# Turning h with VectorE and DRAM in place of TensorE transposes, with the pieces in another order

## The chip, the cores and the metric

The kernel runs on one core of one Trainium2 chip. The metric is the device time of one execution in microseconds. The 32 inputs of the batch are called graphs. "Per graph" is the period of the steady state, read from the starts of equal instructions in neighbouring graphs.

## The reference

Two layers, each with a residual and a layer normalisation, over 32 graphs of 512 nodes with 512 features, all in fp32:

```python
# layer 0: graph convolution, W = [Wi | Wj]
out = deg[None, :, None] * (x @ Wi.T + b) + einsum('ij,bjo->bio', a, x @ Wj.T)
h = layernorm(x + out)
# layer 1: attention over the edges, 8 heads of 64
q, k, v = (split_heads(h @ W.T + bias) for W, bias in ...)
scores = where(adj == 0, -inf, q @ k^T / 8)
out = softmax(scores) @ v
y = layernorm(h + merge_heads(out) @ Wo.T + bo)
```

The step at issue lies between the layers. q, k and v contract over the features of h, so they need h with the features on the partitions; layer 0 leaves it with the nodes there. h has to be turned.

## The kernel before

Every 512x512x512 product is done in seven quarter products (`piece` 1 to 7) instead of eight. Some pieces take a quarter of their operand as it is (1, 2, 3), the others a sum of quarters that GpSimd has made (`combos`: t1 for piece 5, t2 for 6, t3 for 7, t4 for 4). Below, l0-3 is piece 3 of layer 0, pj is the projection by Wo, and v1, q5 and so on are pieces of v and q. Piece by piece, two PSUM banks ("mma" and "mmb") take turns. The copy or sum that takes a finished piece out of its bank is its eviction.

The kernel is a software pipeline in which all engines work in program order. While the attention of graph n-1 runs in eight steps, the pieces of other graphs fill the steps: layer 0, then v, q and k of graph n, pj of graph n-2, and the start of layer 0 of graph n+1. A step is cut from one list by weights; an entry made with `z` weighs nothing, as it is work for the other engines:

```python
def by_steps(todo):
    total, done, at, res = sum(f[0] for f in todo), 0.0, 0, []
    for step in range(STEPS):                       # 8
        res.append([])
        while at < len(todo) and (done < total * (step + 1) / STEPS - 1e-6 or step == STEPS - 1):
            res[-1].append(todo[at]); done += todo[at][0]; at += 1
    return res
# main loop, cut
for step in range(STEPS):
    scores(b, hp, 2 * half); scores(b, hp, 2 * half + 1)   # TensorE; ScalarE exp; VectorE mask product -> e
    ... values(b, ph, phalf) ...; sums(b, ph)              # TensorE, with the e of the step before
    for f in PERIODS[n][step]:
        run(f)                                             # a piece, or a z entry
        ...                                                # after a piece: reciprocals, scale, check, sum of e
```

Two things follow for every step. The two mask products of its `scores` come first in VectorE's order, ahead of everything that the step's list gives to VectorE. And what they make is read by TensorE only in the next step. "e" is the exponentials of the scores times the edge mask; its sum is the denominator of the softmax, and the "check of sums" is a VectorE instruction on these denominators.

h was turned in the kernel before by TensorE, four 128x128 transposes for each of four row groups, through a PSUM tile that is also one of the two score tiles:

```python
def l0_norm(b, ic):
    y = XT[b][:, ic, :]
    if ic == 0:
        HT[b] = big()
    pt = turn_tile()
    for dc in range(DC):
        nc.tensor.transpose(pt[:, dc * P:(dc + 1) * P], y[:, dc * P:(dc + 1) * P], ident)
    nc.scalar.copy(HT[b][:, :, ic * P:(ic + 1) * P], pt.rearrange("p (c i) -> p c i", c=DC))
```

x was already turned by VectorE in 32x32 blocks, with a load from DRAM (`load_xa`) that puts each block where its transpose belongs.

## Time and profile before

| | before |
|---|---|
| median time | 3837.6 us |
| span of the profiled run | 3835.8 us |
| TensorE busy | 99% |
| one graph, by starts | 117.64 us |
| transposes of h on TensorE per graph, by starts | 1.82 us |

How to read the lines in this document. PE is TensorE, DVE VectorE, ACT ScalarE, POOL GpSimd; L339 is line 339 of that run's kernel. In the groups by shape, the columns are line, engine, operation, output and inputs, shapes and count, then busy time and mean length in ns, then the idle time just before and what ended it. In the timeline they are start, length, engine, line, operation and count, with the idle time before it and its releaser in brackets. Matmuls overlap, so the price of one on TensorE is the distance of starts and not its length. From the groups of the kernel before, the ScalarE copy after the transposes and the turn of x on VectorE:

```profile
L339 ACT COPY big<-sc 128x512 f32<-128x512 f32 x128 | 72.0, 592 | 150.9 <-PE sc L338 150.9
L324 DVE STREAM_TRANSPOSE big<-xa 128x512 f32<-128x512 f32 x124 | 85.6, 691 | 0.0
```

512 columns on VectorE cost 0.69 us beside TensorE, while the way through TensorE also costs ScalarE 0.59 us per row group.

### The profile page before, as it was taken

How to read it: one execution, taken by the hardware profiler on the slowest of the kernel's cores; microseconds unless marked ns; L12 is line 12 of the kernel's file. 1: busy time of each engine (PE TensorE's matmuls, PEld its weight loads, DVE VectorE, ACT ScalarE, POOL GpSimd, SP SyncE). 2: the span in 40 equal slices, each digit the busy share in tenths (PEclk: the TensorE clock that was granted, in tenths of full speed). 3: DMA queues.
4: the chain of work that ended last, by engine and by line, in shares of the span. 5: the costliest groups of instructions: out<-in, count | busy, mean ns of one | idle time of the engine just before them, and what ended most of it. 6: DMA issues, size and time to landing. Idle time of an engine off the chain costs nothing.

```text
span 3835.8 us, 46277 instructions
## 1 busy us (share of the span) xinstructions
PE 3794.4 (99%) x16906; PEld 2595.5 (68%) x16906; DVE 2587.3 (67%) x3520; ACT 1064.0 (28%) x1476; POOL 1990.0 (52%) x1985
## 2 busy tenths in 40 slices
PE   8999999999999999999999999999999999999997
PEld 5666767676767676667666666667666767676663
DVE  4667666676766666666767676676667676666765
ACT  2222232222332223322223222232222232222222
POOL 4455544555545555445555455554555554555523
PEclk9999999999999999999999999999999999999998
DMA  7434444444444344434444443444434444444330
GB/s 250 131 99 130 124 124 123 118 113 124 126 124 127 99 129 124 127 120 110 121 128 119 127 126 105 124 127 122 129 99 129 126 121 124 123 111 121 116 110 32
DMA packets 537798, 466.33 MB, mean 122 GB/s; under 512 B 279008, under 2 KB 375776, under 8 KB 537568
## 3 DMA queue, kind: packets, MB, share of 16 engines
q1 hardware_dynamic: 537312, 462.78, 41.7%
q8 instruction: 138, 2.26, 0.2%
q14 instruction: 92, 0.75, 0.1%
q0 software_dynamic: 256, 0.53, 0.0%
HBM read 421.80 MB, written 41.42 MB: 121 GB/s over the span
## 4 chain that ended last, share of the span: by engine, by line
PE 92%; DVE 5%; ACT 1%; DMA 1%; issue 1%; POOL 0%; SPq 0%; POOLq 0%; DVEq 0%; ACTq 0%
PE mmb L393 29%; PE mma L393 29%; PE sc L445 12%; PE ov L466 11%; PE mmb L310 3%; PE mma L310 3%; PE ov L473 3%; DVE e L450 2%; PE sc L338 1%; DVE st L274 1%; DVE es L458 1%; ACT sc L449 1%; DVE rl L488 1%; DVE xh L411 0%; DVE mv L275 0%
## 5 line engine op out<-in xcount | busy, mean ns | idle before, releaser
L449 ACT ACTIVATE sc<-sc 128x1024 f32<-128x1024 f32 x512 | 492.9, 1007 | 1357.2 <-PE sc L445 1353.0
L450 DVE TENSOR_TENSOR e<-sc,edge 128x1024 f32<-128x1024 f32 x512 | 602.5, 1218 | 374.6 <-ACT sc L449 374.6
L393 PE MATMUL mmb<-ring,big 128*128 128x256 f32 x3144 | 728.6, 380 | 0.2 <-ACT big L339 0.2
L393 PE MATMUL mma<-ring,big 128*128 128x256 f32 x3112 | 721.4, 380 | 4.9 <-ACT p L400 3.0
L393 PEld LDWEIGHTS mmb<-ring,big 128*128 128x128 f32 x3144 | 593.8, 190 | 105.5 <-issue 25.9
L393 PEld LDWEIGHTS mma<-ring,big 128*128 128x128 f32 x3112 | 587.6, 190 | 110.2 <-issue 25.2
L362 POOL TENSOR_TENSOR big<-big 128x512 f32<-128x512 f32 x376 | 524.8, 1424 | 205.7 <-ACT big L316 165.0
L445 PE MATMUL sc<-q,k 64*128 64x512 f32 x2048 | 509.7, 616 | 0.0
L466 PE MATMUL ov<-e,v 128*64 128x512 f32 x2048 | 496.1, 605 | 5.8 <-DVE oT L498 5.8
L488 DVE RECIPROCAL rl<-ov 128x128 f32<-128x128 f32 x512 | 459.3, 928 | 15.3 <-PE ov L473 6.0
L393 PE MATMUL mma<-big,ring 128*128 128x256 f32 x1808 | 434.4, 383 | 1.4 <-DVE k L436 0.2
L393 PE MATMUL mmb<-big,ring 128*128 128x256 f32 x1776 | 427.1, 383 | 2.1 <-DVE k L427 0.8
L276 POOL TENSOR_SCALAR mv<-mv 128x1 f32<-128x1 f32 x256 | 49.5, 193 | 724.2 <-DVE mv L275 714.0
L325 POOL TENSOR_TENSOR big<-big,deg_r 128x512 f32<-128x512 f32 x124 | 157.4, 1269 | 512.4 <-DVE big L324 512.4
L393 PEld LDWEIGHTS mma<-big,ring 128*128 128x128 f32 x1808 | 337.2, 190 | 83.2 <-issue 24.3
L393 PEld LDWEIGHTS mmb<-big,ring 128*128 128x128 f32 x1776 | 330.9, 190 | 84.5 <-issue 26.0
L466 PEld LDWEIGHTS ov<-e,v 128*64 128x64 f32 x2048 | 124.6, 136 | 345.9 <-issue 270.8
L456 POOL TENSOR_TENSOR es<-e 128x1024 f32<-128x1024 f32 x128 | 301.7, 2357 | 76.9 <-PE ov L473 63.8
L458 DVE TENSOR_TENSOR es<-es,e 128x1024 f32<-128x1024 f32 x248 | 319.5, 1288 | 0.0
L445 PEld LDWEIGHTS sc<-q,k 64*128 64x128 f32 x2048 | 176.7, 186 | 207.9 <-issue 207.9
L193 POOL TENSOR_TENSOR xlo<-xh,xhi 128x512 fp32r<-128x512 f32 x128 | 163.4, 1287 | 213.3 <-ACT xhi L192 213.3
L408 POOL TENSOR_TENSOR xh<-xh,p 128x512 f32<-128x512 f32 x186 | 231.8, 1273 | 45.8 <-ACT sc L449 39.0
(147 smaller groups left out, 3702.0 us busy)
## 6 DMA issues: line engine op xcount, KB each, us to landing
ring<-wq SPq DMA_DIRECT2D x160, 256.0 KB, 2.7
ring<-wv SPq DMA_DIRECT2D x160, 256.0 KB, 2.6
ring<-wk SPq DMA_DIRECT2D x160, 256.0 KB, 2.8
ring<-wi SPq DMA_DIRECT2D x155, 256.0 KB, 2.8
ring<-wj SPq DMA_DIRECT2D x155, 256.0 KB, 2.6
ring<-wo SPq DMA_DIRECT2D x155, 256.0 KB, 2.6
xh<-in_x_dram SPq DMA_DIRECT2D x32, 1024.0 KB, 5.4
xa<-in_x_dram SPq DMA_DIRECT2D x124, 256.0 KB, 3.8
```

Source lines behind the costliest of these rows:

```text
L193: nc.gpsimd.tensor_sub(lo, xs, hi.bitcast(FT))
L310: nc.tensor.matmul(pm, parts[w][:, jc, :], adjR[:, jc, :], start=(w == 0 and jc == 0), stop=(w == 1 and jc == NC - 1))
L362: nc.gpsimd.tensor_tensor(dst, p, q, op=OP.subtract)
L393: nc.tensor.matmul(pm[:, c * Q:(c + 1) * Q], lhs, rhs, start=first, stop=(kc == 1 and n == len(terms) - 1), skip_group_check=True)
L408: nc.gpsimd.tensor_tensor(d, d, p1, op=OP.add)
L445: nc.tensor.matmul(ps[:, s, :], KT[b, hp // 2][r, hp % 2, kc * P:(kc + 1) * P], QT[b, hp // 2][r, hp % 2, :], start=True, stop=True)
L449: nc.scalar.activation(ps, ps, AF.Exp, scale=QSCALE)
L450: nc.vector.tensor_tensor(e, ps, edge[:, kc:kc + 1, :].to_broadcast([P, 2, N]), op=OP.mult)
L456: nc.gpsimd.tensor_add(ES[hp], E[0], E[1])
L458: nc.vector.tensor_add(ES[hp], ES[hp], E[half])
L466: nc.tensor.matmul(PV[hp][s * HD:(s + 1) * HD, :], V[b][:, kc, c0:c0 + HD], E[kc][:, s, :], start=(kc == 0), stop=(kc == NC - 1))
L488: nc.vector.reciprocal(rl[:, c], pl[:, c])
```

## The change

The intent is to take the transposes off TensorE, the bound engine. From graph 2 on, each normalised half of h (256 rows) is stored to DRAM by the ScalarE queue, loaded back by four transfers that put every 32x32 block in its place, and turned by VectorE with one instruction of 1024 columns. That way is long, so the pieces are put in an order in which work stands between the end of layer 0 and the first piece that needs h. The turns and loads of x move to later steps.

```diff
+    def h_store(b, half):
+        if half == 0:
+            HR[b] = dram.tile([N, D], FT, name="hd", bufs=2)
+        nc.scalar.dma_start(rows(HR[b])[:, 2 * half:2 * half + 2, :], XT[b][:, 2 * half:2 * half + 2, :])
+
+    def h_load(b, half):
+        if half == 0:
+            HA[b] = work([P, DC, N], "xa", 1).rearrange("p (n c) (d i) -> p n (c d) i", n=2, d=2)
+        src = HR[b].rearrange("(t p) (c q f) -> q p c t f", p=32, q=4, f=32)
+        for q in range(4):
+            nc.sync.dma_start(HA[b][32 * q:32 * q + 32, half].rearrange("p c (t f) -> p c t f", f=32),
+                              src[q][:, :, 8 * half:8 * half + 8, :])
+
+    def h_turn(b, half):
+        if half == 0:
+            HT[b] = big()
+        nc.vector.transpose(HT[b][:, :, Q * half:Q * half + Q], HA[b][:, half])
...                                     (piece: the bias of q and k at another visit, because of the new order)
+    LATE = (5, 3, 6, 7, 4)
...                                     (start of layer 0: k in the order LATE, the turns of x here)
 phase_b, graphs 2 to 31:
+        return [l0[2], *project(m, 1), l0[6], *project(m, 2), l0[7], z(add_bo, n - 1, 0), *project(m, 6), l0[4], z(stats, n, 0),
+                *project(m, 7), z(apply, n, 0), z(h_store, n, 0), l0[5], z(add_bo, n - 1, 1), *project(m, 4), z(h_load, n, 0),
+                l0[3], z(stats, n, 1), z(stats, m, 0), *project(m, 5)]
 phase_c, graphs 2 to 31:
+            res = [z(h_turn, n, 0), z(apply, n, 1), z(h_store, n, 1), v[1], *project(m, 3), z(stats, m, 1), v[2], q[1],
+                   z(h_load, n, 1), k[1], z(apply, m, 0), z(apply, m, 1), q[2], z(store, m), k[2], z(h_turn, n, 1),
+                   z(combos, TH, n, h, (1, 2)), z(combos, TH, n, h, (3, 4))]
...                                     (then q and v in the order LATE, with the loads of the next x)
```

More of the change, by code (lines that the diff above doesn't have):

```diff
@@ L96, in turn_tile @@
         return sc_tile()[:, 0, :]
+    HA, HR = {}, {}
     XT, XA, XD, AX_T, HT, MV = {}, {}, {}, {}, {}, {}
@@ L411, in piece @@
                 nc.vector.tensor_tensor(d, d, pm, op=OP.add)
-        elif kind == "v":
-            if i == 1:
-                V[b] = work([P, NC, D], "v", 2)
-            d = quarter(V[b], n, f)
-            if i == 2:
-                nc.scalar.copy(d, pm)
-            elif i in (6, 7, 4):
-                nc.vector.tensor_tensor(d, pm, p1, op=OP.add)
-            elif i != 1:
-                nc.vector.tensor_tensor(d, d, pm, op=OP.add)
-        else:
-            T, bias = (QT, bq_c) if kind == "q" else (KT, bk_c)
-            if i != 1 and (b, f) not in T:
-                T[b, f] = work([P, 2, N], kind, 3)
-            if i in (6, 7):
-                nc.vector.tensor_tensor(T[b, f][:, :, Q * n:Q * n + Q], pm, p1, op=OP.add)
-            elif i != 1:
-                for c in range(2):
-                    d = T[b, f][:, c, Q * n:Q * n + Q]
-                    bc = bias[:, 2 * f + c:2 * f + c + 1]
-                    if i == 2:
-                        nc.scalar.activation(d, pm[:, c, :], AF.Identity, bias=bc, scale=1.0)
-                    else:
-                        o = p1[:, c, :] if i == 4 else d
-                        nc.vector.scalar_tensor_tensor(d, pm[:, c, :], bc, o, op0=OP.add, op1=OP.add)
@@ new lines, in piece @@
+        else:
+            new = (kind, b, f, n) not in OPEN
+            OPEN[kind, b, f, n] = True
+            if kind == "v":
+                if i == 1:
+                    V[b] = work([P, NC, D], "v", 2)
+                d = quarter(V[b], n, f)
+                if i == 2:
+                    nc.scalar.copy(d, pm)
+                elif i != 1:
+                    nc.vector.tensor_tensor(d, pm, p1 if new else d, op=OP.add)
+                return
+            T, bias = (QT, bq_c) if kind == "q" else (KT, bk_c)
+            if i == 1:
+                return
+            if (b, f) not in T:
+                T[b, f] = work([P, 2, N], kind, 3)
+            d = T[b, f][:, :, Q * n:Q * n + Q]
+            if i != 2 and not new:
+                nc.vector.tensor_tensor(d, pm, d, op=OP.add)
+                return
+            for c in range(2):
+                bc = bias[:, 2 * f + c:2 * f + c + 1]
+                if i == 2:
+                    nc.scalar.activation(d[:, c], pm[:, c, :], AF.Identity, bias=bc, scale=1.0)
+                else:
+                    nc.vector.scalar_tensor_tensor(d[:, c], pm[:, c, :], bc, p1[:, c, :], op0=OP.add, op1=OP.add)
@@ L527, in phase_a @@
         if n == B:
-            return [pc("k", n - 1, i, bank) for i, bank in ((6, K), (7, K), (5, A), (4, K), (3, A))]
+            return [pc("k", n - 1, i, bank) for i, bank in ((6, K), (5, A), (7, K), (3, A), (4, K))]
         xq, aq = lambda j, m: quarter(XD[n], j, m), lambda j, m: quarter(AX_T[n], j, m)
         g = [(GA, l0_gather, n, dc, A) for dc in range(DC)]
-        k = [pc("k", n - 1, i, K) for i in ORDER[2:]]
+        k = [pc("k", n - 1, i, K) for i in LATE]
         res = []
         for i in range(DC):
-            res += g[i:i + 1] + k[i:i + 1]
-            if n + 1 < B:
-                res += [z(load_xa, n + 1, i)]
+            res += g[i:i + 1] + k[i:i + 1] + [z(l0_turn, n, i)]
             if n == 1 and i in (1, 3):
@@ L593, in phase_b @@
             return res + [z(apply, n, 0), z(stats, n, 1), (TR, l0_norm, n, 0), (TR, l0_norm, n, 1)]
-        res = project(m, 1)
-        for i in ORDER[1:]:
-            res.append(pc("l0", n, i, banks(n)[0]))
-            if i == 4:
-                res.append(z(stats, n, 0))
-            if i == 5:
-                res.append(z(stats, m, 0))
-            if i == 3:
-                res += [z(stats, n, 1), (TR, l0_norm, n, 1)]
-            res += project(m, i)
-            if i == 4:
-                res.append(z(apply, n, 0))
-            if i == 5:
-                res.append((TR, l0_norm, n, 0))
-            if i in (7, 4):
-                res.append(z(add_bo, n - 1, int(i == 4)))
-        return res
+        A = banks(n)[0]
+        l0 = {i: pc("l0", n, i, A) for i in ORDER}
+        return [l0[2], *project(m, 1), l0[6], *project(m, 2), l0[7], z(add_bo, n - 1, 0), *project(m, 6), l0[4], z(stats, n, 0),
+                *project(m, 7), z(apply, n, 0), z(h_store, n, 0), l0[5], z(add_bo, n - 1, 1), *project(m, 4), z(h_load, n, 0),
+                l0[3], z(stats, n, 1), z(stats, m, 0), *project(m, 5)]
     def phase_c(n):
@@ L617, in phase_c @@
         A, K = banks(n)
-        res = [pc("v", n, 1, A)] + ([z(apply, n, 1)] if n else []) + [pc("q", n, 1, K)]
-        if m >= 0:
-            res += [z(stats, m, 1)]
-        res += [pc("v", n, 2, A), norm[2], norm[3], z(combos, TH, n, h, (1, 2)), pc("k", n, 1, A),
-                z(combos, TH, n, h, (3, 4)), pc("q", n, 2, K), pc("k", n, 2, A)]
+        v, q, k = [{i: pc(kind, n, i, bank) for i in ORDER} for kind, bank in (("v", A), ("q", K), ("k", A))]
+        if m < 0:
+            res = [v[1]] + ([z(apply, n, 1)] if n else []) + [q[1], v[2], norm[2], norm[3], z(combos, TH, n, h, (1, 2)), k[1],
+                                                             z(combos, TH, n, h, (3, 4)), q[2], k[2]]
+        else:
+            res = [z(h_turn, n, 0), z(apply, n, 1), z(h_store, n, 1), v[1], *project(m, 3), z(stats, m, 1), v[2], q[1],
+                   z(h_load, n, 1), k[1], z(apply, m, 0), z(apply, m, 1), q[2], z(store, m), k[2], z(h_turn, n, 1),
+                   z(combos, TH, n, h, (1, 2)), z(combos, TH, n, h, (3, 4))]
         side = []
@@ L626, in phase_c @@
             side = [z(graph_forms, 2), None, z(graph_forms, 0), None, z(graph_forms, 1)]
-        if m >= 0:
-            res += [z(apply, m, 0), z(apply, m, 1), z(store, m)]
-        for i in ORDER[2:]:
-            for f in pc("q", n, i, K), pc("v", n, i, A):
+        for i in LATE:
+            for f in q[i], v[i]:
                 res += [f] + [g for g in side[:1] if g]
                 side = side[1:]
-            if i == 7 and 0 < n < B - 1:
+                if i in (6, 7) and 0 < n < B - 1:
+                    res += [z(load_xa, n + 1, 2 * (i == 7) + (f is v[i]))]
+            if i == 3 and 0 < n < B - 1:
                 res += [z(load_x, n + 1)]
-            if n + 1 < B and i != 3:
-                res += [z(l0_turn, n + 1, (6, 7, 4, 5).index(i))]
-            if i == 5 and n + 1 < B:
+            if i == 7 and n + 1 < B:
                 res += [z(ahead, n + 1)]
```

## The prediction

> **What bounds the kernel now.** I read the busy shares first, then the waits of TensorE, then one period of the timeline. One graph of the batch of 32 takes 117.64 us (the same projection block comes back at 2023.60 and 2141.24 us in the chain of waits), and 29 such periods make up most of the 3837.59 us. The page and the groups by shape say:
>
> ```profile
> PE 3794.4 (99%) x16906; PEld 2595.5 (68%) x16906; DVE 2587.3 (67%) x3520; ACT 1064.0 (28%) x1476; POOL 1990.0 (52%) x1985
> ...
> L338 PE MATMUL sc<-ident,xh 128*128 128x128 f32 x512 | 73.5, 276 | 0.6 <-ACT xh L281 0.3 <-DVE e L450 0.2
> ```
>
> TensorE is busy 99% and no other engine is above 68%, so TensorE sets the time. The second line is what the change attacks: 16 transposes of h per graph. A duration of 276 ns overlaps its neighbour's, so the price is read from starts instead. Here is TensorE, VectorE, GpSimd and ScalarE around two of the transposes (columns: start, length, engine, line, operation, operands, count, idle time before it and its releaser):
>
> ```profile
> 2011.35 1.99 PE L445 MATMUL sc<-q,k 64*128 64x512 f32 x8
> 2013.27 1.94 PE L466 MATMUL ov<-e,v 128*64 128x512 f32 x8
> 2015.03 1.03 PE L473 MATMUL ov<-es,ones 128*64 128x512 f32 x4
> 2015.99 1.99 PE L393 MATMUL mma<-ring,big 128*128 128x256 f32 x8
> 2017.82 3.62 PE L393 MATMUL mmb<-ring,big 128*128 128x256 f32 x16
> ...
> 2023.00 0.60 PE L338 MATMUL sc<-ident,xh 128*128 128x128 f32 x4
> 2023.44 3.62 PE L393 MATMUL mmb<-ring,big 128*128 128x256 f32 x16
> 2026.99 1.99 PE L445 MATMUL sc<-q,k 64*128 64x512 f32 x8
> 2028.91 1.94 PE L466 MATMUL ov<-e,v 128*64 128x512 f32 x8
> 2030.77 0.66 PE L338 MATMUL sc<-ident,xh 128*128 128x128 f32 x4
> ```
>
> ```profile
> 2026.88 0.69 DVE L498 TENSOR_TENSOR oT<-ov,rl 128x512 f32<-128x512 f32 x1
> 2027.49 0.68 DVE L411 TENSOR_TENSOR xh<-xh,mmb 128x512 f32<-128x512 f32 x1
> ...
> 2029.20 2.36 DVE L450 TENSOR_TENSOR e<-sc,edge 128x1024 f32<-128x1024 f32 x2 [0.37 <-ACT sc L449]
> ```
>
> From starts: four transposes take 0.44 us (2023.00 to 2023.44), a small piece of 8 matmuls 1.73, a layer-0 piece of 16 3.46, an attention block 3.8 (4.64 with the four sums). The period is eight steps, each an attention block followed by about 10.4 us of pieces. VectorE reaches the mask products (L450) only 2.2 us after the block begins and ends them 4.57 us after it (2026.99 to 2031.56), 0.8 us later than TensorE is through the block. In the kernel before that harms nothing: the next block needs them, not the next piece.
>
> **What the Trainium skill says.** "TensorE: Matmul & The Clock Gate", Part 4, gives about 275 ns for a transpose in a kernel's context; the trace agrees (276), but its starts show that only 110 ns of that is occupied. "VectorE: DVE Perf Modes", The three transpose paths, says VectorE turns 32x32 blocks only, which is why the change needs DRAM to put blocks in place; L324 in this trace, a 128x512 one, takes 691 ns. "DMA: Bandwidth & Descriptors", Two DMAs through the same engine are not ordered, says that the issuer must wait for the first transfer's completion before a dependent one; no run yet shows it for h. "TensorE: Matmul & The Clock Gate", Part 1, says that an idle window of about 3.4 us halves TensorE's clock until it has been busy again as long. The trace agrees: near the end two 512-column matmuls (L691) occupy 0.96 us normally, but 1.87 after an idle stretch of 4.22 us; the blocks up to 3804.50 lose about 2.6 us together. After idle stretches of 2.17 and 3.01 us nothing was lost.
>
> ```profile
> 3785.49 1.13 PE L691 MATMUL mma<-xh,oT 128*128 128x512 f32 x2
> 3786.45 1.02 PE L691 MATMUL mmb<-xh,oT 128*128 128x512 f32 x2
> ...
> 3798.05 2.07 PE L691 MATMUL mma<-xh,oT 128*128 128x512 f32 x2 [4.22 <-DVE oT L498]
> 3799.92 1.92 PE L691 MATMUL mmb<-xh,oT 128*128 128x512 f32 x2
> ```
>
> **The change part by part.** It acts for graphs 2 to 31, so 30 times; graphs 0 and 1 keep their transposes.
>
> Removed: 16 transposes (0.44 + 0.50 + 0.88 = 1.82 us of TensorE per graph by their starts), and four ScalarE copies of 0.59 us, which were hidden. The most that can be gained is 30 x 1.82 = 55 us, 1.4%.
>
> Added, DMA: per graph 1 MB stored in two halves and loaded in two halves of four transfers, with runs of 128 bytes. A similar load of x (256 KB, L110) costs 0.59 us to issue and lands in 3.8; a 1 MB store lands in 5.2. Four loads then land some 4 x 0.59 + 3.8 = 6.2 us after the first issue. The 254,005 packets of this size took 207 us on each of 16 engines in the trace, so 246,000 more add some 5% to a 42% load. That is bandwidth to spare.
>
> Added, VectorE: two turns of 1024 columns per graph. By L450, whose 1024 columns run at about 1.2 us, I put them at 1.2 us each. VectorE has 67% in use, so the sum does not matter; their place in its order does, because engines work in program order. I cut the new list of pieces into the eight steps by the kernel's own weights (80.26 in total, 10.03 a step), with the parts interleaved as the main loop does.
>
> First half of h. Step 2 holds l0-5, pj4, load, l0-3, pj5; the turn opens step 3, after the mask products, and v1 needs it. With step 2 at 0, TensorE ends l0-5 at 8.2, pj4 at 9.9, l0-3 at 13.4, pj5 at 15.2, and the block of step 3 at 19.0. The store goes out at about 5 and lands before 9; the load is issued at 10 and landed at about 16. DMA is in time. VectorE is not. After l0-3 it has in order: eviction 0.6, a reciprocal 0.85, scale 0.6, statistics of four row groups 3.2 (two rows took 1.6 at 2015.84), pj5's eviction 0.6, the check of sums 0.75. From 13.55 that ends at 20.15. Then two mask products (2.36) to 22.5 and the turn (1.2) to 23.7. TensorE has wanted v1 since 19.0: **a new wait of about 4.75 us**, of which 2.0 would be there even with an empty VectorE queue.
>
> Second half. From the resumed v1 (23.75), seven pieces end at 34.3, the block and sums of step 4 at 39.0 and k2 at 40.8. ScalarE now has four normalisations (2.9 us) ahead of q2's eviction and the exponentials, so these end near 39; mask products near 40.2, one reciprocal 41, turn 42.2. GpSimd has its sum of e (2.35 us, after the mask products) ahead of the first combination (1.27): 43.75. q5, the very next piece, needs that combination: **a second wait of about 3 us**, 2 if ScalarE's delay is smaller than I think.
>
> Moved: the turns of x come later (steps 6 and 7), with 5 us of GpSimd products. Adding up steps 7 and 0, GpSimd has the combinations for l0-6 about 10 us before they are needed. I count nothing. Biases are only added at another visit: the same number of VectorE instructions.
>
> Clock: an idle stretch of 4.75 us holds a whole free-running window of 3.4 us in about (4.75 - 3.4) / 3.4 = 40% of the cases. At 2.6 us each that is an estimated 1.0 us per graph, using that window from the skill.
>
> Sum per graph: -1.82 + 4.75 + 3.0 + 1.0 = +6.9 us; times 30 is +208 us, 4045 us. As every term of mine could be too long by some tenths, and the order may hide a part, I say 4030.
>
> **The rivals.**
> First, all hidden: about 3785 us. For it: DMA is in time, TensorE is otherwise the bound, and the order was visibly made to leave time. Against it: the turn cannot pass the mask products queued before it, and these end 0.8 us after TensorE's block even in an undisturbed step.
> Second, one small wait only: if the backlog at the end of step 2 is absent, the waits are 2 + 2 us, minus 1.8, about +65 us, 3905. Against it: four row groups of statistics now stand between l0-3 and the mask products.
> Third, the load becomes the wait: if 128-byte transfers beside the weight loads take 12 us rather than 6, the first half still lands at 22, before VectorE is free; the second half would hardly be later than 42. So DMA should not be what shows, and if it shows the time goes above 4100.
> Fourth, GpSimd becomes the bound in steps 7 and 0, with some microseconds at l0-6: it is 52% busy and I found slack.
>
> **Range and chances.** The small case gives 3905, both full waits without clock loss 3837 - 55 + 30 x 7.75 = 4015, with the clock lost in every graph 4093. Hence 3930 to 4110. Faster by over 2% is beyond what the removed work can give. Within 2% needs a net loss under 2.5 us per graph (77 / 30), i.e. most of the first wait hidden: 11%.
>
> **What would show it.** Right: in a period of the new trace, TensorE idle or waiting at its first matmuls after the attention block of step 3, released by the VectorE transpose of h; a second gap before the piece after k2, released by GpSimd's combination; a period of 122 to 126 us instead of 117.6; matmuls of double length after the long gap in some periods. VectorE should start the turn directly after L450, not after waiting for a DMA. Wrong: a period near 115.8; the transpose waiting for the load; or the gap at another piece, which would mean that my cut into steps or the order of VectorE's work is not the real one.

## The result, and the profile after

The changed kernel is correct and takes 4146.88 us (4144.12 to 4153.82, four runs) against 3837.63. The ratio is 1.0807 (95% interval 1.0788 to 1.0825).

The page of the changed kernel begins with the busy shares:

```profile
PE 3881.7 (93%) x16426; PEld 2653.3 (64%) x16426; DVE 2695.3 (65%) x3580; ACT 989.1 (24%) x1356; POOL 2027.5 (49%) x1985
```

TensorE has 480 matmuls fewer (30 graphs of 16), but it is idle 7% of the span and its busy time has risen by 87 us. Both need a cause. Here is TensorE in one graph of the changed kernel, around the first pieces that need h:

```profile
2054.80 1.99 PE L467 MATMUL sc<-q,k 64*128 64x512 f32 x8
2056.72 1.94 PE L488 MATMUL ov<-e,v 128*64 128x512 f32 x8
2063.37 3.75 PE L413 MATMUL mma<-ring,big 128*128 128x256 f32 x8 [4.71 <-issue]
2066.92 2.34 PE L413 MATMUL mmb<-ring,oT 128*128 128x256 f32 x8
2069.09 1.89 PE L413 MATMUL mma<-ring,big 128*128 128x256 f32 x8
...
2080.74 1.99 PE L413 MATMUL mma<-big,ring 128*128 128x256 f32 x8
2085.67 3.78 PE L413 MATMUL mmb<-big,ring 128*128 128x256 f32 x8 [2.94 <-POOL big L382]
2089.25 3.11 PE L413 MATMUL mma<-ring,big 128*128 128x256 f32 x8
```

The third line is v1. It should have started 1.87 us after the line above it, at 2058.59; it starts 4.78 us later. The line of 2085.67 is q5. It should have followed k2 (2080.74) after 1.83 us; it is 3.10 us late. And the piece after each gap is slow: v1 takes 3.55 us from start to start instead of 1.83, pj3 2.17 instead of 1.73, q5 3.58 and v5 2.95. The profile names no engine for the first gap ("issue"), so VectorE's own timeline has to be read beside it:

```profile
2055.38 0.69 DVE L275 BATCH_NORM_STATS2 st<-xh 128x6 f32<-128x512 f32 x1
...
2058.58 0.65 DVE L431 TENSOR_TENSOR xh<-xh,mmb 128x512 f32<-128x512 f32 x1
2059.16 0.69 DVE L515 CUSTOM_DVE_ANT_0 ov<-ov,rl 128x512 f32<-128x512 f32 x1
...
2059.76 2.35 DVE L472 TENSOR_TENSOR e<-sc,edge 128x1024 f32<-128x1024 f32 x2
2062.03 1.24 DVE L359 STREAM_TRANSPOSE big<-xa 128x1024 f32<-128x1024 f32 x1
```

VectorE runs without a pause: four rows of statistics from 2055.38 to 2058.58, pj5's eviction, the check of sums, the two mask products, and only then the turn of h (L359), which ends at 2063.27. v1 starts 0.10 us later. The turn has no wait for a transfer in front of it. For the second gap GpSimd shows the same picture:

```profile
2082.05 2.35 POOL L478 TENSOR_TENSOR es<-e 128x1024 f32<-128x1024 f32 x1 [7.57 <-DVE e L472]
2084.36 5.04 POOL L382 TENSOR_TENSOR big<-big 128x512 f32<-128x512 f32 x4
```

The sum of e (L478), which waited for late mask products, is ahead of the combinations of h's quarters (L382). q5 starts when the first of these four is done. But the sum was not the main delay. VectorE's turn of h's second half, queued behind the mask products and a reciprocal, itself ended only at 2083.87 (L359, 2082.68 + 1.19), and the sum at 2084.40 (2082.05 + 2.35). Without the sum, the first combination could have begun some 0.5 us earlier, an estimate from these ends.

The slow pieces have their own view. These are stretches of the changed kernel as long as the clock's own steps in this trace, 3.41 us; the columns are the stretch, its length, TensorE's busy time and number of matmuls, the granted clock, DMA share and GB/s:

```profile
2057.58:2060.99 3.41, 1.08 (x6) 1.00 0.18 70
2060.99:2064.41 3.42, 1.04 (x3) 0.50 0.29 111
2064.41:2067.82 3.41, 3.41 (x10) 0.50 0.00 0
...
2081.47:2084.89 3.42, 1.26 (x6) 1.00 0.63 215
2084.89:2088.30 3.41, 2.63 (x6) 0.50 0.00 1
2088.30:2091.71 3.41, 3.41 (x9) 0.50 0.20 76
```

After a stretch in which TensorE worked for only 1.08 us, and again after one of 1.26 us, the clock is halved for two stretches (in every other graph for one only after the second gap). This happens at both gaps, in every graph from 2 to 31. The steady period is 128.0 us (v1 at 1807.35 and 2063.37, two graphs apart: 256.02), so a graph costs 10.4 us more than before, and 30 x 10.36 = 311 us is the whole difference of 309.

### The profile page after: what moved, and what is told of

Its sections match the earlier page's. It is cut to its first block, busy times and chain, and to the rows that moved or that the text cites. A ratio compares the mean times of both kernels' runs of the same rounds, so it can differ in the third digit from the quotient of the medians.

```text
span 4152.1 us, 46000 instructions
## 1 busy us (share of the span) xinstructions
PE 3881.7 (93%) x16426; PEld 2653.3 (64%) x16426; DVE 2695.3 (65%) x3580; ACT 989.1 (24%) x1356; POOL 2027.5 (49%) x1985
## 4 chain that ended last, share of the span: by engine, by line
PE 85%; issue 4%; DVE 4%; ACT 4%; POOL 3%; DMA 0%; SPq 0%; ACTq 0%; POOLq 0%; DVEq 0%
PE mma L413 28%; PE mmb L413 28%; PE sc L467 10%; PE ov L488 10%; PE mmb L311 3%; PE mma L311 3%; ACT xh L282 2%; PE ov L495 2%; DVE e L472 2%; POOL es L478 2%; POOL big L382 1%; ACT sc L471 1%; ACT q L456 1%; DVE rl L510 0%; PE ov L505 0%
## 5 line engine op out<-in xcount | busy, mean ns | idle before, releaser
L413 PE MATMUL mma<-ring,big 128*128 128x256 f32 x3112 | 770.4, 399 | 74.7 <-issue 70.8
L413 PE MATMUL mmb<-ring,big 128*128 128x256 f32 x3144 | 759.4, 392 | 74.7 <-issue 72.2
L413 PEld LDWEIGHTS mma<-ring,big 128*128 128x128 f32 x3112 | 617.4, 200 | 219.3 <-issue 98.2
L194 POOL TENSOR_TENSOR xlo<-xh,xhi 128x512 fp32r<-128x512 f32 x128 | 215.3, 1692 | 736.6 <-ACT xhi L193 736.6
L382 POOL TENSOR_TENSOR big<-big 128x512 f32<-128x512 f32 x376 | 507.4, 1377 | 28.6 <-ACT big L340 12.0
L413 PE MATMUL mma<-big,ring 128*128 128x256 f32 x1808 | 455.0, 397 | 45.4 <-POOL big L382 44.7
L413 PE MATMUL mmb<-big,ring 128*128 128x256 f32 x1776 | 451.0, 399 | 44.1 <-POOL big L382 44.1
L478 POOL TENSOR_TENSOR es<-e 128x1024 f32<-128x1024 f32 x128 | 301.9, 2359 | 339.9 <-DVE e L472 219.5
L413 PEld LDWEIGHTS mmb<-big,ring 128*128 128x128 f32 x1776 | 349.2, 199 | 126.5 <-POOL big L382 50.1
L480 DVE TENSOR_TENSOR es<-es,e 128x1024 f32<-128x1024 f32 x248 | 357.8, 1443 | 0.0
L431 DVE TENSOR_TENSOR xh<-xh,mma 128x512 f32<-128x512 f32 x186 | 126.0, 677 | 277.4 <-PE mma L413 276.8
L431 DVE TENSOR_TENSOR xh<-xh,mmb 128x512 f32<-128x512 f32 x186 | 126.0, 677 | 254.9 <-PE mmb L413 254.8
```

Of the source, the lines that this page charges most:

```text
L194: nc.gpsimd.tensor_sub(lo, xs, hi.bitcast(FT))
L382: nc.gpsimd.tensor_tensor(dst, p, q, op=OP.subtract)
L413: nc.tensor.matmul(pm[:, c * Q:(c + 1) * Q], lhs, rhs, start=first, stop=(kc == 1 and n == len(terms) - 1), skip_group_check=True)
L431: nc.vector.tensor_tensor(d, d, pm, op=OP.add)
L478: nc.gpsimd.tensor_add(ES[hp], E[0], E[1])
L480: nc.vector.tensor_add(ES[hp], ES[hp], E[half])
```

## The experiments

All edits are against the changed kernel. All eight kernels were timed beside the kernel before on the same chip (median 3837.3 to 3837.4 there); all are correct except the one that says otherwise. The theory is that TensorE waits first for VectorE's turn behind its queue, then for GpSimd's combination behind its own, and that each wait then costs again through the clock. The main rivals are that the trip through DRAM is what comes late, and that the slow pieces have another cause.

### Keeping TensorE busy in the gaps

```diff
+        for _ in range({("v", 1): 10, ("q", 5): 6}.get((kind, i), 0) if b > 1 else 0):
+            nc.tensor.matmul(pm[:, 0:Q], ones, deg_r[:, 0:Q], start=True, stop=True, skip_group_check=True)
```

> The changed kernel with dummy matmuls in the two waits of TensorE: ten ones-by-deg_r products (256 columns, fp32) into v1's own accumulator ahead of v1 and six ahead of q5, all overwritten. They fill 10 x 0.43 = 4.3 us of the first wait and 6 x 0.43 = 2.6 us of the second, so the waits themselves stay as long as before (4.78 and 3.10 us by the starts), but TensorE never idles for long. Theory (waits as predicted, and the half clock follows from the idleness in them): the half-clock stretches go, 4.9 us per graph on average, 147 us in all: about 4000 us. Rival (the slow matmuls after the gaps are slow for another reason, such as weight loads arriving late or memory traffic): no change, 4140 to 4150, or more because of the added work.

Measured: 4008.29 us (4006.65 to 4011.18), ratio to before 1.0444 (1.0427 to 1.0462). From TensorE's timeline of this run, the dummies (L408; the trace counts each of these products twice) and v1:

```profile
1990.05 4.58 PE L408 MATMUL mma<-deg_r,ones 128*128 128x256 f32 x20
1994.79 1.99 PE L415 MATMUL mma<-ring,big 128*128 128x256 f32 x8
1996.62 1.89 PE L415 MATMUL mmb<-ring,oT 128*128 128x256 f32 x8
```

v1 comes 4.74 us after the dummies begin, as late as without them, but v1 and pj3 now take 1.83 and 1.72 us. The period is 123.14 us (v1 at 1994.79 and 2117.93). Adding useless work made the kernel 139 us faster. So the slow pieces follow from TensorE's idleness and not from the lateness of its operands, and the clock is worth 128.0 - 123.1 = 4.9 us per graph.

### Without the trip through DRAM

```diff
-            HR[b] = dram.tile([N, D], FT, name="hd", bufs=2)
-        nc.scalar.dma_start(rows(HR[b])[:, 2 * half:2 * half + 2, :], XT[b][:, 2 * half:2 * half + 2, :])
+            HR[b] = x[b]
+        h_load(b, half)
 ... and both z(h_load, ...) entries taken out of the list
```

> The changed kernel with h's loads reading x from DRAM instead of the stored h (wrong result on purpose), without the store and issued at the place of the store, several us earlier; same bytes, same transfers, same turns. Theory (the first wait is VectorE's order, the second GpSimd's behind it; the loads land with some 5 and 2.6 us to spare): within 10 us of the changed kernel, 4137 to 4157, gaps before v1 and q5 still 4.7 and 2.9 us. Rival (the trip through DRAM is what TensorE waits for): the gaps shrink or go and the time falls by 100 us or more, below 4050.

Measured: 4148.26 us (4146.63 to 4150.13), and a wrong result. The gaps before v1 and q5 are still there:

```profile
1037.60 3.75 PE L413 MATMUL mma<-ring,big 128*128 128x256 f32 x8 [4.71 <-issue]
1059.95 2.50 PE L413 MATMUL mmb<-big,ring 128*128 128x256 f32 x5 [3.00 <-POOL big L382]
```

In the order of the changed kernel, the store, the wait for it and the time of the load are not on the path. In the changed kernel itself, the last of the four loads of the first half is issued by 2053.44 and lands some 3.5 us later (the median of these loads), about 2056.9, while the turn begins at 2062.03.

### The first turn ahead of the mask products

```diff
-  z(h_store, n, 0), l0[5], z(add_bo, n - 1, 1), *project(m, 4), z(h_load, n, 0),
-  l0[3], z(stats, n, 1), z(stats, m, 0), *project(m, 5)]
+  z(h_store, n, 0), l0[5], z(h_load, n, 0), z(add_bo, n - 1, 1), *project(m, 4),
+  l0[3], z(h_turn, n, 0), z(stats, n, 1), z(stats, m, 0), *project(m, 5)]
-            res = [z(h_turn, n, 0), z(apply, n, 1), ...
+            res = [z(apply, n, 1), ...
```

> The changed kernel with the turn of h's first half moved in VectorE's order from behind the mask products to straight behind layer-0 piece 3 (ahead of the four rows of statistics), and its load moved one piece earlier so that it is there. Nothing else moves. Theory: the gap before v1 (4.7 us) and the half clock after it (2.5 us) go; the backlog now delays pj3's eviction and may cost about 1 us before q1; the second gap stays. 30 x (7.3 - 1) = 190 us less: 3930 to 3970. Rival (the backlog only moves and appears as an equal wait one or two pieces later, or the turn waits for the load): above 4060.

Measured: 3942.39 us (3936.62 to 3949.06), ratio 1.0268 (1.025 to 1.0285). The two idle stretches of a graph are now these:

```profile
1120.02 1.99 PE L413 MATMUL mma<-big,ring 128*128 128x256 f32 x8 [0.88 <-DVE xh L431]
1134.97 2.59 PE L413 MATMUL mma<-big,ring 128*128 128x256 f32 x8 [2.94 <-POOL big L382]
```

The gap before v1 is gone. The queue that remains on VectorE shows up as the expected small wait for pj3's eviction, 0.88 us. The second gap is untouched. Moving one entry in VectorE's order, with its load a piece earlier, gave back 204 us of the 309.

### Both turns in a better place

The same move, and for the second half:

```diff
+            res = [z(apply, n, 1), z(h_store, n, 1), v[1], *project(m, 3), z(stats, m, 0), z(stats, m, 1), v[2], z(h_load, n, 1),
+                   q[1], k[1], z(h_turn, n, 1), z(combos, TH, n, h, (1, 2)), q[2], k[2], z(combos, TH, n, h, (3, 4)),
+                   z(apply, m, 0), z(apply, m, 1), z(store, m)]
```

(stats of graph m's first half also leaves its place behind l0-3.)

> The changed kernel with both turns moved ahead of the mask products in VectorE's order (the second with its first two combinations ahead of q2, so ahead of GpSimd's sum of e), the loads one piece earlier, statistics of the older graph behind pj3, its normalisation behind k2. Theory (only the two waits and the clock loss stand between the change and its gain): period 117.6 - 1.8 = 115.8 us, 3783 us, at most 3800 with small new waits. Rival (the new order or the added DMA and VectorE work costs more than the two places): above 3838, so no gain over the kernel before.

Measured: 3770.59 us (3766.38 to 3772.87), ratio 0.9824 (0.9807 to 0.984). This version beats both kernels: 1.8% faster than the kernel before, which is under the 2% that I call faster, but clear of noise. Its VectorE in the order of time, around the first turn, and two whole graphs of it in the windows view (length, then busy time and number of instructions of TensorE, weight loads, VectorE, ScalarE and GpSimd, then clock and DMA):

```profile
2108.07 0.69 DVE L520 TENSOR_TENSOR oT<-ov,rl 128x512 f32<-128x512 f32 x1
2108.68 1.24 DVE L359 STREAM_TRANSPOSE big<-xa 128x1024 f32<-128x1024 f32 x1
...
2112.60 2.35 DVE L472 TENSOR_TENSOR e<-sc,edge 128x1024 f32<-128x1024 f32 x2
```

```profile
1990.00:2105.20 115.20, 115.20 (x513) 79.71 (x512) 83.20 (x111) 30.95 (x42) 62.07 (x62) 1.00 0.52 142
2105.20:2220.40 115.20, 115.20 (x514) 79.72 (x513) 83.30 (x111) 30.95 (x42) 62.53 (x62) 1.00 0.52 142
```

The turn now stands before the mask products and ends at 2109.92; v1 starts on time at 2111.89. The mask products end at 2114.95, 6.85 us after their step began (2108.10). In the kernel before they ended 4.57 us after the beginning of theirs (2026.99 to 2031.56). Being 2.3 us later harms nothing, as only the next step reads them. TensorE is busy from end to end of both graphs. The trip through DRAM has less room in this order: VectorE is idle for 2.58 us before the turn of the second half (2123.60), which waits for its load; the turn is still done 4.07 us before q5 begins (2124.85 and 2128.92). The period is 115.20 us, 2.44 less than before: more than the 1.82 us that the transposes were thought to be worth.

### The better order with TensorE's transposes

```diff
 the order of the run above, and
+    def h_store(b, half): pass
+    def h_load(b, half): pass
+    def h_turn(b, half):
+        for ic in range(2 * half, 2 * half + 2):
+            l0_norm(b, ic)
```

> The order of the run with both turns moved (e4_both), but h turned by TensorE as in the kernel before (two groups of four transposes at each place of a turn, their ScalarE copies, no store, no load). It splits the gain of e4_both (2.44 us a graph by its period of 115.20 us against 117.64) into the transposes and the order of the pieces. Theory (the transposes are worth the 1.82 us that their starts show, and the order some 0.6 us, which were small waits ahead of pieces whose accumulator was still being emptied): period 117.0, about 3818 us (3812 to 3826). Rival (all 2.44 us belong to the transposes and what they disturb): 3835 to 3842, or slower.

Measured over five rounds: 3818.06 us (3815.08 to 3821.42), ratio 0.995 (0.9936 to 0.9964). Eight of the transposes, in two neighbouring graphs:

```profile
2013.05 1.04 PE L339 MATMUL sc<-ident,xh 128*128 128x128 f32 x8
...
2130.00 1.04 PE L339 MATMUL sc<-ident,xh 128*128 128x128 f32 x8
```

They come again after 116.95 us. So of the 2.44 us per graph, 0.69 belong to the order of the pieces (117.64 to 116.95) and 1.75 to taking the transposes off TensorE (116.95 to 115.20). The traces show where most of the 0.69 was: with equally many matmuls in a graph, the starts of the pieces' matmuls (L393, here L404) were 0.64 us further apart in sum in the kernel before.

### Less of VectorE's queue

```diff
-                l0[3], z(stats, n, 1), z(stats, m, 0), *project(m, 5)]
+                l0[3], z(stats, n, 1), *project(m, 5)]
-   ... v[1], *project(m, 3), z(stats, m, 1), ...
+   ... v[1], *project(m, 3), z(stats, m, 0), z(stats, m, 1), ...
```

> The changed kernel with the two rows of statistics of the older graph moved from behind layer-0 piece 3 to behind pj3 (after v1); the turn stays behind the mask products. Theory (the first wait is the sum of VectorE's backlog): 1.6 us less backlog, so the gap before v1 goes from 4.7 to 3.1 us, the second gap stays 2.9; the half clock may follow both gaps as before or less often. 30 x 1.6 = 48 us less with the same clock: 4098, and down to 4050 where the clock recovers earlier. Rival (the wait is set by something else, such as the store and load): gap unchanged at 4.7, about 4147.

Measured: 4079.22 us with an unusually wide spread (4059.43 to 4101.24), ratio 1.0612 (1.0576 to 1.0648). TensorE's first gap, v1:

```profile
1529.77 3.11 PE L413 MATMUL mma<-ring,big 128*128 128x256 f32 x8 [3.12 <-issue]
```

1.6 us of statistics less on VectorE make the gap 1.59 us shorter (4.71 to 3.12): the first wait is VectorE's queue, microsecond for microsecond. The clock of the four runs was not equally good (0.959 in the run of 4101.24, 0.970 in that of 4059.43), so the spread goes with the clock; why the runs differ in it was not looked into.

### ScalarE's normalisations later

```diff
-  z(h_load, n, 1), k[1], z(apply, m, 0), z(apply, m, 1), q[2], z(store, m), k[2], z(h_turn, n, 1),
+  z(h_load, n, 1), k[1], q[2], k[2], z(apply, m, 0), z(apply, m, 1), z(store, m), z(h_turn, n, 1),
```

> The changed kernel with the four normalisations of the older graph (2.9 us of ScalarE) moved from ahead of q2's eviction and the exponentials to behind k2's eviction. Theory (ScalarE's delay of the exponentials is one part of the second wait, the other is the reciprocal, the turn and GpSimd's sum of e in a row): the gap before q5 goes from 2.9 to about 1.9 us, the first stays 4.7. 30 x 1.1 = 33 us less, 4114, and down to 4050 if the clock is no longer halved after the second gap. Rival (GpSimd alone sets it): gap unchanged, 4147.

Measured: 4034.64 us (4033.76 to 4036.11), ratio 1.0512 (1.0495 to 1.053). TensorE's second gap, q5:

```profile
1532.95 1.99 PE L413 MATMUL mmb<-big,ring 128*128 128x256 f32 x8 [1.81 <-POOL big L382]
```

The gap falls from 2.94 to 1.81 us and q5 is no longer slow. The time is 15 us below the lowest that I had expected (4050); that half microsecond per graph was not followed up. A gap 1.1 us shorter was worth 112 us, or 3.7 us per graph: below some length a gap no longer halves the clock.

### How much idleness halves the clock

Half the dummies of the first experiment: five before v1 and three before q5.

> As e1_warm, with half as many dummy matmuls (five before v1, three before q5), at the start of each wait: about 2.6 and 1.8 us of idleness are left. It tells what idleness halves the clock. In the two traces so far every window of 3.41 us with at least 1.99 us idle was followed by half clock, and none with up to 1.62 us was (first microseconds left out). Theory (a window that is idle for somewhat more than half is enough): half clock still follows the first gap in part of the graphs or all, rarely the second: 4030 to 4100. Rival (the window has to be idle from end to end, as I assumed in the prediction): as e1_warm, 4000 to 4015.

Measured: 4034.68 us (4031.31 to 4039.66), ratio 1.0513 (1.0495 to 1.053): 26 us more than with all the dummies. TensorE is idle for 2.3 us before v1 and 1.66 us before q5, and the clock was halved 15 times in the run (64 times in the changed kernel, 3 times with all the dummies). Here is v1; its wait is now put down to the turn of h (L359) by the profile itself:

```profile
1511.73 1.99 PE L415 MATMUL mma<-ring,big 128*128 128x256 f32 x8 [2.31 <-DVE big L359]
```

I cut all ten traces into windows of 3.413 us at the edges of their half-clock stretches and took TensorE's idle time in each, by the modelled ends of matmuls, the first microseconds left out. Every window at full clock that was followed by half clock had at least 1.97 us idle (272 of them in the nine traces besides that of the kernel before; 2 in that). Of the windows not followed by it, the idlest had 2.01. The step lies at about 2.0 us. A window need not be idle from end to end.

The run with only the first turn moved shows most plainly that the share within one window decides. Its second gap has the same length (2.94 us) in 29 graphs, at changing places in the windows. In the 22 graphs in which half clock followed, 1.97 to 2.52 us of the gap lay in one window; in the seven others, at most 1.55 to 2.00.

## Why the prediction was wrong

It put 4030 us in a range of 3930 to 4110, and 4146.88 was measured. The direction and both waits held; the cost of the clock after them did not. Per graph, in its own terms:

| term | predicted, us | measured, us | from |
|---|---|---|---|
| transposes off TensorE | -1.82 | -1.75 | the two runs in the better order, 116.95 and 115.20 |
| order of the pieces | 0 | -0.69 | 117.64 and 116.95 |
| first wait, v1 for VectorE's turn | +4.75 | +4.78 | starts in the changed kernel |
| second wait, q5 for GpSimd's t1 | +3.0 | +3.10 | starts in the changed kernel |
| half clock after the waits | +1.0 | +4.9 | 128.0 and 123.1, the run kept busy |
| sum | +6.9 | +10.3 | 128.00 - 117.64 = 10.36 |

- **The step that failed** is the clock: "an idle stretch of 4.75 us holds a whole free-running window of 3.4 us in about (4.75 - 3.4) / 3.4 = 40% of the cases". The runs show that about 2.0 us idle within one window is enough. A gap of 4.71 us of idleness lies across windows of 3.41 in such a way that one of them always has at least 2.35 us of it, so the first wait is charged in every graph, not in 40%. The second wait was charged nothing in the prediction, because it is shorter than a window; at 2.94 us of idleness it puts 2.0 us into one window in about seven of ten random positions (an estimate from these lengths; 22 of 29 in the run with only the first turn moved). In the changed kernel it did so every time. Even the prediction's highest case, 4093 us, charged one loss of 2.6 us per graph; two losses, together 4.9 us, were measured. The half clock ends at an edge of a window (2067.82), and from there to the second gap lies a fixed piece of work, so the position is not random; that this is why it is every time is my argument from the edges, not tested.
- **The prediction's own evidence.** Nothing was lost after an idle stretch of 3.01 us, which misled me: it lay across an edge with 1.5 us on either side. But the same trace could have shown the error. Its stretch of 4.22 us held no whole window: the window before that half clock (3793.19 to 3796.60) has TensorE busy for 0.64 us. And the window before the next one (3817.07 to 3820.48) has it busy for 1.38 us, so idle for only 2.03.
- **The first wait** came out as its sum: VectorE's instructions stood in the order listed, the turn began directly behind the mask products, and 1.6 us less of the queue took 1.59 us off the gap.
- **The second wait** came out in size and in its releaser. ScalarE's normalisations are 1.1 us of it, by the run that moved them. GpSimd's sum of e is only some 0.5 us of it by the ends read above, and no run took it away alone; the rest is the chain on VectorE (mask products, reciprocal, turn) and the combination itself. The prediction's times say the same when looked at closely: its turn ends at 42.2, and the sum of e ends at about 42.5 (40.2 + 2.35). It also counts seven pieces up to 34.3, but its time is that of six, and the trace has six.
- **The trip through DRAM** was in time, as predicted; the run without the store has the same gaps and, within 2 us, the same time. In the better order the second turn does wait for its load, but TensorE doesn't.
- **The moved turns of x** cost nothing that shows: once the two waits are gone, TensorE is busy throughout the graph.
- **The most to be gained** was put too low, at 1.4%. It is 1.8%, because the new order also ended small waits, 0.69 us per graph, which the prediction did not look for in the kernel before. That the total was not missed by more is in part luck: this gain was not foreseen.
- The rivals: all hidden, one small wait only, the load as the wait and GpSimd as the bound in layer 0 were all refuted, the first only for the order as it was written.

## What to carry to other kernels

When work is moved to an engine that executes in program order, its place in that engine's queue can count for more than its cost, as it did here: list what stands ahead of it between its operands and its user, and put it ahead of work that only the next step needs. Price every new wait of TensorE twice, once for its length and once for the clock after it, as soon as some two microseconds of it can fall into one window of 3.41 us; below that, a wait cost only itself in these runs. If a change with a sound idea comes out slower, cut the waits it made before giving it up: here the same idea went from 8% slower to 1.8% faster by moving a few entries of a list.

## What the Trainium skill lacked or had wrong

- "TensorE: Matmul & The Clock Gate", Part 1, gives "≥1 idle window (~3.4µs)" as what halves the clock, and the page's table under "Why this matters for your kernels" allows gaps up to about 3 us. The length of the window agrees (stretches of 3.41 and 6.83 us in the records), but "idle" is too strict: windows with 1.97 us idle of 3.41 were followed by half clock, and 2.01 was the most that was not. Gaps of 2.94 us (3.50 in the last graph) were followed by it in all 30 graphs of the changed kernel, gaps of 2.94 us in 22 of 29 graphs of another, and gaps of 2.3 us in 10 of 29 of a third. Windows with less than 1.97 us idle were never followed by it in these runs; the page gives no such share.
- The same page, HAM oscillation, tells of gaps that halve the clock again and again and puts the loss at half of the throttled time. Here 390 us of half clock against 28 in the run that was kept busy would give 181 us by that rule; 139 were measured (144 between the two profiled runs). TensorE is still idle in a part of the throttled time (2.38 us of 6.83 after the first gap), and that part costs nothing more: the likely reason why the rule comes out too high here.
